# Four layers in one kernel: the second block's attention part in four parts of 256 tokens, its routing in two halves, and the first experts' weights asked for from the counts

## The chip, the core and the metric

The kernel is one program on one core of a Trainium2 chip. A core has five engines with a queue each: TensorE (PE, with its weight loads as PEld) multiplies 128 x 128 blocks into PSUM, VectorE (DVE) and ScalarE (ACT) work elementwise and read PSUM, GpSimd (POOL) works on SBUF and issues the gathers, SyncE (SP) issues most other transfers. Each executes its own queue in order and waits on semaphores for the others. The metric is the device time of one execution in microseconds (us).

## The reference, cut to what matters

x is 16 batches of 64 tokens with 256 features, 1024 tokens in all. Four layers follow one another, each a cross-attention, a second mixing step and a feed-forward step, each added to x:

```python
x = x + _L1_xattn_ref(_layernorm(x), ctx_768, ...)
x = x + _L1_attn_ref(_layernorm(x), ...)
x = x + _L1_ffn_ref(_layernorm(x), ...)
x = x + _L2_xattn_ref(_layernorm(x), ctx_768, ...)
```

The change lies in the second and third of these lines. `_L1_attn_ref`, on its normalized input:

```python
h = _ln(x, ln_conv_g, ln_conv_b)
x = x + conv(h) + conv_b                      # 4 steps back in time, groups of 64 features
h = _ln(x, ln_attn_g, ln_attn_b)
q, k, v = h @ Wq.T + bq, h @ Wk.T + bk, h @ Wv.T + bv
pooled_q = cumsum(q) / (1, 2, ... S)
pooled_k = cumsum(pooled_q * k) / (1, 2, ... S)
x = x + pooled_k * v
h = _ln(x, ln_boom_g, ln_boom_b)
return x + gelu(h @ Wb.T + bb) @ Wu.T + bu
```

`_L1_ffn_ref` sends each token to one of eight experts, the one with the largest softmax probability of `x @ router_W + router_b`: `gate * (relu(x @ W1[e] + b1[e]) @ W2[e] + b2[e])`, with 1024 hidden features. Nothing in either step mixes one batch with another, except that the experts' blocks are filled from all tokens.

## The kernel before

**Layout.** `xs` holds x as eight tiles of 128 tokens x 256 features. TensorE contracts over partitions, so a product needs its input turned to features first: `transposed` (L175) makes two 128 x 128 transposes per tile into PSUM, and another engine evicts them. A float32 product is two instructions in the trace, a transpose is one.

**The stage around the change.** `L1_attn` (L1489) takes each step for all eight tiles before the next step. `norm_x` (L184) normalizes the tiles into `htok` and also evicts their transposes to `hT`, which `L1_attn` does not read. `norm` (L163) does a second normalization into `lnw`, transposes it, and VectorE scales and shifts it into `hp`, which has three columns of zeros ahead of each batch (L1503). The convolution (`ps_conv`, L1514) runs in 512-column products, is turned back and added (`add_by_features`, L1522); another `norm` into `hT` (L1537), q, k, v (`ps_qkv`, L1566), the two running means by scans (`running_mean`, L1554), the sum, another `norm`, the two boom matrices (`ps_hid` L1587, `po` L1591). A normalization of a tile is four VectorE instructions, with one GpSimd power between (`norm_tile`, L150).

**Routing and experts.** `L1_ffn` (L1355) normalizes all tiles (`norm_x`), stores the rows to DRAM for the gather (`keep_row`, L1088, in SP's queue), computes logits (L1010), softmax, the chosen expert, each token's place among those of its expert (`route` L1092, `ranks` L1223). `blocks` (L1245) turns the counts into `rows`, which says where the weights of each block of 128 tokens lie, and with the table of tokens into `tokens`, which says which rows a block gathers. Then eight products add the gate-weighted biases `b2` (L1366 to L1373). Each block (L1374) asks GpSimd for its two weight matrices `wa` and `wb` by `rows` (L1345) and for its tokens `hb` by `tokens` (L1325), three gathers in GpSimd's queue, with three buffers each. Fourteen blocks always run, further ones if the counts need them.

**What sets the order.** Inside `manual_schedule` the named engines' instructions stand in the order of the program text; all other orders are made by a planner with a cost for each instruction. `L1_xattn` before this stage orders TensorE by hand; `L1_attn` and `L1_ffn` are planned throughout. Tiles come from pools; a tile that reuses the memory of an earlier one waits for its readers. `psm` is the PSUM pool of `misc` tiles (two here), `lps` the pool for a layer's own shapes. Weights come through `pack` (L104) into two alternating slots of a ring: attention's weights, the boom matrices, the router's weights with b2 (`pack_L1_gate`), then the next layer's; each pack is asked for when the one before it is taken up.

## Time and profile before

| | us |
|---|---|
| median of 3 runs (2992.84 to 3002.1) | 2994.78 |
| the profiled execution, its own time | 2998.29 |
| its span on the core | 2996.5 |
| attention part, from its first transposes to the last sum into `xs` | 998.35 to 1144.8 |
| logits end, first gather of weights, experts' first transposes | 1158.4, 1172.40, 1189.27 |
| experts' fourteen blocks, end about | 1302 |

Over the span PE is busy 2700.2 us (90%), DVE 1482.1 (49%), ACT 1022.7 (34%), POOL 308.7 (10%); the mean granted TensorE clock is 0.948. These shares are averages over stages with different limits, so the stage from 998 to 1189 has to be read by itself. In the stretches of the trace shown below the first pair is start and end in us from the start of the span, then the length, then the busy time and instruction count of PE, PEld, DVE, ACT and POOL, then the granted clock (1.00 is full speed), the share of the DMA engines that is busy, and GB/s. In the groups, the part between the bars is busy time in us and mean ns of one; the last part is the idle time of the engine ahead of them and what ended it.

### The profile page before, as it was taken

The numbers are of one execution on the slowest core, as the hardware profiler recorded it, in microseconds if no ns is written. First come the engines' busy times: TensorE is split into PE (matmuls) and PEld (weight loads), VectorE is DVE, ScalarE is ACT, GpSimd is POOL, SyncE is SP. The second block draws the span as 40 slices with busy tenths as digits, with TensorE's granted clock in tenths as the row PEclk, the third lists the DMA queues.
The fourth block names the chain that finished last, engine by engine and source line by source line (L and its number), as shares of the span: only waits on it lengthen the run. The fifth ranks groups of instructions, "written<-read, shape, count | busy, mean of one in ns | idle before, by whom it ended". The sixth has DMA issues, their size and how long they took to land. (4 is left out here: it accounts for less than half of the span.)

```text
span 2996.5 us, 42608 instructions
## 1 busy us (share of the span) xinstructions
PE 2700.2 (90%) x16840; PEld 1952.8 (65%) x16840; DVE 1482.1 (49%) x3177; ACT 1022.7 (34%) x2290; POOL 308.7 (10%) x428
## 2 busy tenths in 40 slices
PE   7888997999999788989999998898998898897899
PEld 3566784666666345867777776795776666665668
DVE  3654114666666653234444444314445747658581
ACT  2331122555555211222333322122334455445330
POOL 1112223000000111310101001101001000000000
PEclk9987997999999897989999999899999999998999
DMA  9503771101101003831121112551112222121210
GB/s 241 177 27 144 263 239 50 40 26 32 30 26 33 29 8 135 294 76 46 45 66 45 43 58 70 199 212 63 52 51 88 64 62 73 57 68 53 57 36 7
DMA packets 79220, 253.55 MB, mean 85 GB/s; under 512 B 15151, under 2 KB 26954, under 8 KB 69290
## 3 DMA queue, kind: packets, MB, share of 16 engines
q1 hardware_dynamic: 59562, 165.01, 17.7%
q0 software_dynamic: 13312, 80.28, 7.9%
q10 hardware_dynamic: 6144, 5.51, 0.5%
q8 instruction: 134, 2.20, 0.3%
q14 instruction: 68, 0.56, 0.1%
HBM read 233.80 MB, written 14.82 MB: 83 GB/s over the span
## 5 line engine op out<-in xcount | busy, mean ns | idle before, releaser
L223 DVE TENSOR_REDUCE nmx<-sc 128x1 f32<-128x1024 f32 x264 | 311.8, 1219 | 219.6 <-PE sc L507 134.6
L225 ACT ACTIVATE p<-sc,nmx 128x1024 f32<-128x1024 f32 x264 | 294.6, 1116 | 316.9 <-DVE nmx L223 316.2
L507 PE MATMUL sc<-ctxT,qp 128*128 128x512 f32 (+1 forms) x1024 | 356.0, 602 | 0.0
L507 PEld LDWEIGHTS sc<-ctxT,qp 128*128 128x128 f32 (+1 forms) x1024 | 139.0, 190 | 154.0 <-issue 153.4
L69 PE MATMUL halves<-ctx,pT 128*128 128x192 f32 x1024 | 191.6, 344 | 9.4 <-DVE xs L89 4.0
L69 PEld LDWEIGHTS halves<-ctx,pT 128*128 128x128 f32 x1024 | 179.1, 203 | 12.3 <-DVE xs L89 4.5
L160 POOL TENSOR_TENSOR ln_rs<-ln_ve,nhalf 128x1 f32<-128x1 f32 x120 | 66.9, 562 | 1134.1 <-DVE ln_ve L158 1025.5
L69 PE MATMUL misc<-ctx,pT 128*128 128x192 f32 x1024 | 177.6, 327 | 0.5 <-DVE qT L472 0.5
L235 PE MATMUL ps_t<-ident,p 128*128 128x128 f32 x1088 | 147.8, 278 | 25.3 <-ACT p L225 17.7
L69 PEld LDWEIGHTS misc<-ctx,pT 128*128 128x128 f32 x1024 | 166.3, 191 | 2.1 <-DVE qT L472 1.0
L1938 ACT ACTIVATE da<-rep,al 128x252 f32<-128x252 f32 x256 | 114.7, 498 | 114.8 <-DVE x L1948 98.4
L235 PEld LDWEIGHTS ps_t<-ident,p 128*128 128x128 f32 x1088 | 127.7, 143 | 39.2 <-ACT p L225 22.5
L1948 DVE TENSOR_TENSOR_SCAN x<-da,x 128x512 f32<-128x512 f32 x128 | 152.1, 1213 | 1.9 <-ACT da L1938 1.4
L235 PE MATMUL misc<-ident,p 128*128 128x128 f32 x1024 | 139.8, 283 | 14.2 <-ACT p L225 6.7
L237 ACT COPY pT<-ps_t 128x512 f32<-128x512 f32 x182 | 104.3, 585 | 140.5 <-PE ps_t L235 138.5
L235 PEld LDWEIGHTS misc<-ident,p 128*128 128x128 f32 x1024 | 112.2, 143 | 40.3 <-ACT p L225 13.3
L69 PE MATMUL ps_h<-r,w 128*128 128x256 f32 x512 | 115.3, 385 | 0.0
L237 ACT COPY pT<-misc 128x512 f32<-128x512 f32 x128 | 75.0, 586 | 114.9 <-PE misc L235 114.6
L69 PEld LDWEIGHTS ps_h<-r,w 128*128 128x128 f32 x512 | 97.8, 192 | 16.6 <-issue 2.9
L69 PE MATMUL gu<-dT,wa 128*128 128x128 f32 (+1 forms) x864 | 104.8, 280 | 3.7 <-ACT dT L64 2.4
L239 DVE COPY pT<-misc 128x512 f32<-128x512 f32 x128 | 88.2, 689 | 39.4 <-PE misc L235 28.9
L69 PE MATMUL po<-wb,hid 128*128 128x256 f32 (+1 forms) x440 | 105.6, 387 | 0.0
(472 smaller groups left out, 4437.7 us busy)
## 6 DMA issues: line engine op xcount, KB each, us to landing
ctx<-in_ctx SPq DMA_DIRECT2D x48, 768.0 KB, 4.4
ctxT<-in_ctxT SPq DMA_DIRECT2D x48, 512.0 KB, 4.0
w<-in_L2f_W SPq DMA_DIRECT2D x24, 1024.0 KB, 8.5
rep<-dus SPq DMA_DIRECT2D x256, 64.0 KB, 1.9
ctxT<-in_ctxT SPq DMA_DIRECT2D x16, 768.0 KB, 12.9
ctxT<-in_ctxT SPq DMA_DIRECT2D x96, 128.0 KB, 3.5
ys<-yb ACTq DMA_DIRECT2D x40, 128.0 KB, 4.4
bc_rep<-bcs SPq DMA_DIRECT2D x32, 128.0 KB, 3.0
```

Source lines behind the costliest of these rows:

```text
L69: self.nc.tensor.matmul(out, lhsT, rhs, start=n == 0, stop=n == len(pairs) - 1)
L160: nc.gpsimd.tensor_tensor(rs, ve, self.nhalf, ALU.pow)
L223: self.nc.vector.tensor_reduce(nmx, sc, AX.X, ALU.max, negate=True)
L225: self.nc.scalar.activation(p, sc, AF.Exp, bias=nmx, accum_out=sums)
L235: self.nc.tensor.transpose(ps[:, u, :], p[:, at : at + 128], self.ident)
L237: self.nc.scalar.copy(pT[:, 4 * g : 4 * g + 4, :], ps)
L239: self.nc.vector.tensor_copy(pT[:, 0:4, :], ps)
L507: nc.tensor.matmul(sc[u][:, bass.ts(kh, 512)], qp[n][par][rows, h : h + 2, :].rearrange("p h q -> p (h q)"), ctx[0][rows, at], start=n == ...
L1938: nc.scalar.activation(da[:, g, :, 1:], now[j][:, 0, :].rearrange("p (b s) -> p b s", s=S)[:, :, 1:], AF.Exp, scale=al[:, col : col + 1],)
L1948: nc.vector.tensor_tensor_scan(flat, da.rearrange("p g b s -> p (g b s)"), flat, 0.0, ALU.mult, ALU.add)
```

## The change

`L1_attn` now works on four parts of 256 tokens. Each part is a generator of fifteen steps (`part`), each half of the routing one of five (`routing`), and the string `turns` says whose step comes next: digits 0, 1, 3 and 4 are the four parts, 2 and 5 the routing of the first and the second 512 tokens. TensorE's order is this order (manual). Products have 256 columns. The scale and shift after a normalization, and the biases of k and v, are done by ScalarE during the eviction; a normalization handles two tiles with one GpSimd power. The unread `hT` of the first `norm_x` is gone. `lps` is closed and `misc` has eight PSUM tiles.

Routing, `keep_row` and the bias products move from `L1_ffn` into this layer. `blocks` becomes `block_experts` in two pieces: the first needs only the counts and makes `rows`; it is called after the second half's places have been started and before they are completed. The second makes `tokens`. The first block's weights are gathered by the first `rows`; those of all later blocks by a second tile made from the first and `at`, the lookup's operand. The router's weights load with the boom matrices, and the next layer's weights are asked for at the end of `L1_attn`. Tiles that must outlive the layer move to the `routes` pool. `self.rows` becomes a list with an entry per block. `head` in `pair_masks` shares the memory of `sel`. `gate_bufs`, 4 during `L1_attn`, is the buffer count of the small routing tiles.

```diff
-        head = pool.tile([8, 2, 128], F32, name="head")
-        nc.vector.tensor_copy(head, of)
         mine = pool.tile([8, 2], F32, name="mine")
         sel = pool.tile([8, 2, 2, 128], F32, name="sel")
+        head = sel[:, 1]
+        nc.vector.tensor_copy(head, of)
         for h in range(2):
             nc.vector.tensor_scalar(mine[:, h : h + 1], self.lane[:8], 2.0, float(h), ALU.mult, ALU.add)
             nc.vector.tensor_scalar(sel[:, h], head, mine[:, h : h + 1], None, ALU.is_equal)
...
-    def keep_row(self, i):
-        self.nc.sync.dma_start(self.hs[1 + i * 128 : 1 + (i + 1) * 128], self.htok[:, i, :])
+    def keep_row(self, i, x=None):
+        self.nc.sync.dma_start(self.hs[1 + i * 128 : 1 + (i + 1) * 128], self.htok[:, i, :] if x is None else x)
...
         w2 = self.lp.tile([128, 6 * D], F32, tag="wb" + own, bufs=1 if own else 3, name="wb")
-        self.gather_rows(w2, self.a["L0f_w2r"], self.rows[:, j : j + 1])
+        self.gather_rows(w2, self.a["L0f_w2r"], self.rows[j][:, j : j + 1])
...
@@ -1244,6 +1244,12 @@
     def blocks(self, r, n_blocks):
+        rest = self.block_experts(r, n_blocks)
+        next(rest)
+        next(rest, None)
+    def block_experts(self, r, n_blocks, later=False):
...
-        rows = self.lp.tile([128, n_blocks], I32, name="rows")
+        rows = self.routes.tile([128, n_blocks], I32, tag="rows", name="rows")
         nc.vector.tensor_scalar(rows, of, self.lane, None, ALU.add)
+        self.rows = [rows] * n_blocks
+        yield
         nc.vector.tensor_tensor(past, past, end.unsqueeze(1).to_broadcast(shape), ALU.mult)
         at = self.lp.tile([128, n_blocks], F32, name="at_block")
@@ -1279,18 +1287,25 @@
         nc.vector.tensor_scalar(at, at, self.lane, None, ALU.is_equal)
         ps = self.misc([128, n_blocks])
         self.mm(ps, [(r.table, at[: E * T // 128])])
-        tokens = self.lp.tile([128, n_blocks], I32, name="tokens")
+        tokens = self.routes.tile([128, n_blocks], I32, tag="tokens", name="tokens")
         nc.vector.tensor_copy(tokens, ps)
         first = self.lp.tile([128, E], F32, name="first")
         nc.vector.tensor_tensor(first, end, nb, ALU.subtract)
         nc.vector.tensor_scalar(first, first, 128.0, 1.0, ALU.mult, ALU.subtract)
+        self.tokens = tokens
+        if later:
+            rows = self.routes.tile([128, n_blocks], I32, name="rows_later")
+            behind = self.lp.tile([128, n_blocks], F32, name="behind")
+            nc.vector.scalar_tensor_tensor(behind, at, 0.0, of, ALU.mult, ALU.add)
+            nc.vector.tensor_scalar(rows, behind, self.lane, None, ALU.add)
+            self.rows[1:] = [rows] * (n_blocks - 1)
...
-        return rows, tokens
...
@@ -1335,18 +1350,11 @@
-    def pack_L1_gate(self):
-        self.slot()
-        w, row = self.load("L1f_rW"), self.load_row("L1f_rb")
-        b2 = self.carve(E, D)
-        self.nc.sync.dma_start(b2, self.a["L1f_b2"])
-        return w, row, b2
...
@@ -1354,23 +1362,6 @@
     def L1_ffn(self):
         nc = self.nc
-        rw, rb, b2 = self.pack()
-        self.norm_x()
-        self.routed = r = self.route_setup(1)
-        for i in range(NT):
-            self.keep_row(i)
-        gates = self.gate("gates")
-        for _ in self.route(r, self.gate_logits(rw, rb), 0, gates):
-            pass
-        self.rows, self.tokens = self.blocks(r, L1_BLOCKS)
-        for i in range(NT):
-            pg = self.misc([E, 128])
-            nc.tensor.transpose(pg, gates[:, i, :], self.ident)
-            gT = self.lp.tile([E, 128], F32, tag="gT", bufs=2, name="gT")
-            self.evict(gT, pg)
-            po = self.misc([128, D])
-            self.mm(po, [(gT, b2)])
-            self.add_to_x(i, po)
         def block(j, own=""):
...
@@ -1484,115 +1475,196 @@
     def pack_L1_boom(self):
         self.slot()
-        return self.load("L1a_WbT"), self.load("L1a_WuT"), self.load_row("L1a_bu")
+        boom = self.load("L1a_WbT"), self.load("L1a_WuT"), self.load_row("L1a_bu")
+        gate = self.load("L1f_rW"), self.load_row("L1f_rb")
+        b2 = self.carve(E, D)
+        self.nc.sync.dma_start(b2, self.a["L1f_b2"])
+        return boom, gate, b2
     def L1_attn(self):
         nc = self.nc
-        cv, wq, wk, wv = self.pack()
...
+        (cv, *qkv), ((wb, wu, bu), (rw, rb), b2) = self.pack(), self.pack(ahead=False)
+        self.lps_close()
+        routed, self.gate_bufs = self.route_setup(1), 4
+        later = self.later_steps()
+        def tokens(p, name):
+            return self.lp.tile([128, 2, D], F32, name=f"{name}{p}")
+        def features(p, name):
+            return self.lp.tile([128, 2, CHUNK], F32, name=f"{name}{p}")
+        def normalized(x, out):
+            mv = self.small.tile([128, 2, 2], F32, name="ln_mv2")
+            for t in range(2):
+                st = self.small.tile([128, 6], F32, name="ln_st")
+                nc.vector.bn_stats(st, x[:, t, :])
+                nc.vector.bn_aggr(mv[:, t, :], st)
+            rs = self.small.tile([128, 2], F32, name="ln_rs2")
+            nc.vector.tensor_scalar(rs, mv[:, :, 1], 1e-5, None, ALU.add)
+            nc.gpsimd.tensor_tensor(rs, rs, self.nhalf.to_broadcast([128, 2]), ALU.pow)
+            for t in range(2):
+                nc.vector.tensor_scalar(
+                    out[:, t, :], x[:, t, :], mv[:, t, 0:1], rs[:, t : t + 1], ALU.subtract, ALU.mult
+                )
+        def transposed(x):
+            ps = self.misc([128, 2, CHUNK])
+            for t in range(2):
+                for c in range(2):
+                    nc.tensor.transpose(ps[:, c, bass.ts(t, 128)], x[:, t, c * 128 : (c + 1) * 128], self.ident)
+            return ps
+        def affine(x, to, g, b):
+            ps = transposed(x)
             for c in range(2):
+                src = ps[:, c, :]
+                if len(to.shape) == 4:
+                    src = src.rearrange("p (b s) -> p b s", s=S)
+                nc.scalar.activation(
+                    to[:, c], src, AF.Identity, bias=self.col(b, c), scale=self.col(g, c)
                 )
+        def added(x, to):
+            ps = self.misc([128, 2, D])
+            for t in range(2):
+                for c in range(2):
+                    nc.tensor.transpose(ps[:, t, bass.ts(c, 128)], x[:, c, t * 128 : (t + 1) * 128], self.ident)
+            nc.vector.tensor_tensor(to, to, ps, ALU.add)
+        by_features = [None] * NC
+        def part(p):
+            x = self.xs[:, 2 * p : 2 * p + 2, :]
+            hp = self.lp.tile([128, 2, 4, S + 3], F32, name=f"hp{p}")
+            nc.gpsimd.memset(hp[:, :, :, 0:3], 0.0)
+            x1, w = tokens(p, "x1"), tokens(p, "lnw")
+            normalized(x, x1)
+            normalized(x1, w)
+            yield
+            affine(w, hp[:, :, :, 3:], "L1a_lcg", "L1a_lcb")
+            yield
+            ps = self.misc([128, 2, CHUNK])
+            conv = features(p, "hTs")
             for c in range(2):
                 self.mm(
+                    ps[:, c, :].rearrange("p (b s) -> p b s", s=S),
+                    [(cv[:, c, k, :], hp[:, c, :, k : k + S]) for k in range(4)],
                 )
+            for c in range(2):
+                nc.scalar.activation(conv[:, c, :], ps[:, c, :], AF.Identity, bias=self.col("L1a_conv_b", c))
+            yield
+            added(conv, x1)
+            w = tokens(p, "lnw")
+            normalized(x1, w)
+            yield
+            hT = features(p, "hTs")
+            affine(w, hT, "L1a_lag", "L1a_lab")
+            yield
+            got = []
+            for m, name in zip(qkv, "qkv"):
+                ps = self.misc([128, 2, CHUNK])
+                got.append(features(p, name))
+                for o in range(2):
+                    self.mm(ps[:, o, :], [(m[:, c, o * 128 : (o + 1) * 128], hT[:, c, :]) for c in range(2)])
+                for o in range(2):
+                    nc.scalar.activation(
+                        got[-1][:, o, :], ps[:, o, :], AF.Identity, bias=self.col(f"L1a_b{name}", o)
                     )
+                if name == "q":
+                    yield
+            q, k, v = got
+            inv = self.inv_s.unsqueeze(1).to_broadcast([128, 8, S])
+            for y in (k, v):
+                flat = q.rearrange("p c t -> p (c t)")
+                nc.vector.tensor_tensor_scan(flat, later, flat, 0.0, ALU.mult, ALU.add)
+                steps = q.rearrange("p c (b s) -> p (c b) s", s=S)
+                nc.vector.tensor_tensor(steps, steps, inv, ALU.mult)
+                nc.vector.tensor_tensor(q, q, y, ALU.mult)
+            yield
+            added(q, x1)
+            w = tokens(p, "lnw")
+            normalized(x1, w)
+            nc.gpsimd.tensor_tensor(x, x, x1, ALU.add)
+            yield
+            hT = features(p, "hTs")
+            affine(w, hT, "L1a_lbg", "L1a_lbb")
+            yield
+            if p < 2:
+                g = self.act.tile([128, 8, CHUNK], F32, tag=("htok", "hT")[p], name="hid")
+            else:
+                g = self.lp.tile([128, 8, CHUNK], F32, name=f"hid{p}")
+            for m2 in range(4):
+                ps = self.misc([128, 2, CHUNK])
+                for u in range(2):
+                    m = 2 * m2 + u
+                    self.mm(ps[:, u, :], [(wb[:, c, m * 128 : (m + 1) * 128], hT[:, c, :]) for c in range(2)])
+                for u in range(2):
+                    m = 2 * m2 + u
+                    nc.scalar.activation(g[:, m, :], ps[:, u, :], AF.Gelu, bias=self.col("L1a_bb", m))
+                if m2 % 2:
+                    yield
+            for t in range(2):
                 po = self.misc([128, D])
                 self.mm(
                     po,
                     [(g[:, m, t * 128 : (t + 1) * 128], wu[:, m, :]) for m in range(8)] + [(self.ones[:1, :], bu)],
                 )
+                self.add_to_x(2 * p + t, po)
+                yield
+            o = tokens(p, "x1")
+            normalized(x, o)
+            for t in range(2):
+                self.keep_row(2 * p + t, o[:, t, :])
+            yield
+            by_features[p] = features(p, "hTs")
+            nc.scalar.copy(by_features[p], transposed(o))
+            yield
+        def routing(first):
+            ps = self.misc([128, 4, E])
+            for t in range(4):
+                hT = by_features[(first + t) // 2]
+                self.mm(
+                    ps[:, t, :],
+                    [(hT[:, c, bass.ts(t % 2, 128)], rw[:, c, :]) for c in range(2)] + [(self.ones[:1, :], rb)],
+                )
+            gates = self.gate(f"gates{first}", 4)
+            for piece, _ in enumerate(self.route(routed, ps, first, gates)):
+                if first and not piece:
+                    experts = self.block_experts(routed, L1_BLOCKS, True)
+                    next(experts)
+                yield
+            if first:
+                next(experts, None)
+            yield
+            gTs = []
+            for t in range(4):
+                pg = self.misc([E, 128])
+                nc.tensor.transpose(pg, gates[:, t, :], self.ident)
+                gTs.append(self.lp.tile([E, 128], F32, tag="gT", bufs=4, name="gT"))
+                self.evict(gTs[t], pg)
+            yield
+            for t in range(4):
+                po = self.misc([128, D])
+                self.mm(po, [(gTs[t], b2)])
+                self.add_to_x(first + t, po)
+            yield
+        turns = "0010130134013004314101340301301403101341041134031434234323424242455555"
+        with self.tc.manual_schedule(engines={mybir.EngineType.PE}):
+            parts = [part(0), part(1), routing(0), part(2), part(3), routing(4)]
+            for p in turns:
+                next(parts[int(p)])
+        self.start_pack(self.at)
+        self.routed, self.gate_bufs = routed, 1
...
             "L1_attn": (self.L1_attn, [self.pack_L1_attn, self.pack_L1_boom]),
-            "L1_ffn": (self.L1_ffn, [self.pack_L1_gate]),
+            "L1_ffn": (self.L1_ffn, []),
             "L2_xattn_attn": (self.L2_xattn_attn, [lambda: self.pack_heads64("L2"), self.pack_L2_attn]),
...
                 tc.tile_pool(
-                    name=f"psm_{name}", bufs=3 if name == "L1_xattn" else 2, space=PSUM, reuse_waits="tile"
+                    name=f"psm_{name}", bufs={"L1_xattn": 3, "L1_attn": 8}.get(name, 2), space=PSUM, reuse_waits="tile"
                 ) as self.ps_misc,
```

## The prediction

> **What bounds the kernel now.** I first cut the stage that the diff rewrites into stretches (busy time per engine; the last three numbers are TensorE's granted clock, the DMA share and GB/s). The stage is the second block's attention part and the routing, from 998.3 us to the experts' first instruction at 1189.3.
>
> ```profile
> 998.30:1009.90 11.60, 5.43 (x24) 2.69 (x24) 9.85 (x39) 1.49 (x4) 3.30 (x6) 0.77 0.47 182
> 1009.90:1031.00 21.10, 19.89 (x56) 9.44 (x56) 7.90 (x30) 2.75 (x4) 1.74 (x4) 0.88 0.00 1
> 1031.00:1046.00 15.00, 9.45 (x27) 4.29 (x26) 12.45 (x45) 0.69 (x1) 4.24 (x8) 0.77 0.00 0
> 1046.00:1070.00 24.00, 19.78 (x55) 8.55 (x54) 22.92 (x35) 3.34 (x4) 2.70 (x4) 0.99 0.01 1
> 1070.00:1081.00 11.00, 3.55 (x12) 1.81 (x13) 8.07 (x29) 0.00 (x0) 5.53 (x10) 0.50 0.00 0
> 1081.00:1127.20 46.20, 46.20 (x144) 26.14 (x143) 11.71 (x40) 10.31 (x15) 3.81 (x7) 0.98 0.04 12
> 1144.40:1158.50 14.10, 12.46 (x64) 11.10 (x64) 3.07 (x9) 2.77 (x5) 0.55 (x1) 0.74 0.46 160
> 1158.50:1172.40 13.90, 5.87 (x23) 4.70 (x23) 10.93 (x60) 0.26 (x1) 0.00 (x1) 0.50 0.00 1
> 1172.40:1189.30 16.90, 12.74 (x27) 5.16 (x27) 4.87 (x20) 1.02 (x4) 8.53 (x9) 0.50 0.89 329
> ```
>
> PE (first) and DVE (third) take turns: whenever DVE is near full (1031, 1070, 1158), PE is under two thirds busy and its clock falls to half; while PE is full (1081 to 1127), DVE does a quarter. All 1024 tokens go through each step together, so nothing else can fill a normalization. Next, the groups of instructions, for what PE waits on (last column) and the price of pooling:
>
> ```profile
> L179 PE MATMUL misc<-ident,lnw 128*128 128x128 f32 x48 | 12.8, 372 | 17.9 <-DVE lnw L170 10.7 <-DVE ln_mv L156 3.7 <-DVE ln_ve L158 3.5
> L1556 DVE TENSOR_TENSOR_SCAN pk<-later,pq 128x512 f32<-128x512 f32 x4 | 4.9, 1224 | 0.1
> L1557 DVE TENSOR_TENSOR pk<-pk,inv_s 128x512 f32<-128x512 f32 x4 | 2.8, 692 | 0.1
> ```
>
> Last, the order in time around the experts' start:
>
> ```profile
> 1172.40 1.00 POOL L1312 DMA_INDIRECT wa<-in_L1f_W1b,rows  x1 [25.68 <-DVE first L1286]
> 1175.00 0.95 POOL L1312 DMA_INDIRECT hb<-hs,tokens  x1 [0.36 <-ACT gT L64]
> 1188.12 1.22 PE L69 MATMUL misc<-w,gT 8*128 8x256 f32 x2 [0.40 <-DVE gT L62]
> 1189.27 0.69 PE L179 MATMUL misc<-ident,hb 128*128 128x128 f32 x2
> ```
>
> Weights and tokens are asked for at 1172 to 1175, but the experts start only when PE has finished the eight bias products (`gT`), one every 1.9 us at half clock. Afterwards (1189 to 1302) PE is full; I leave that stage as it is.
>
> **TensorE's work after the change.** Durations are spacings in the trace at full clock: a 512-column pass 0.43 us, a 256-column pass 0.214 (15 weight loads in 3.21 us), a transpose 0.13 (four in about 0.5). Half as many columns per pass costs nothing, since 0.19 us of weight load still fits under 0.214. Each product is two passes.
> - Convolution 64 x 0.214 = 13.7; q, k, v 96 x 0.214 = 20.5; first boom matrix 128 x 0.214 = 27.4; second, eight tiles at 4.27 (1131.43 to 1135.70) = 34.2; transposes 96 x 0.13 = 12.5 (16 fewer: the unused `hT` of L188 goes). Together 108.3, or 27 per part.
> - Routing of the first half: logits four tiles x 0.85 = 3.4, ranks 0.9, table 8 x 0.22 = 1.8, gate transposes 0.4, bias products 2.0: 8.5, between turns of the parts.
> - Logits of the second half, 3.4.
>
> That is 120.2 us up to the end of the last logits, if PE never waited; the stretches above spend 160.1 on it (998.3 to 1158.4).
>
> **Waits that stay.** A two-tile normalization from its input to its output is 3.0 us (one tile: 1131.99 to 1133.96 is 2.0; the second adds 0.6 of statistics and 0.41 of scaling). VectorE's part of it is 2.15.
> - Start: two normalizations in a row for part 0 lie between 998 and its first transpose. They cost 0 if done during the attention before, 6 if not. No tile of this pool was written before 993.62 (`hp`'s memset) or 998.35 (`later`), so I take 5.
> - The next turns of part 0 wait for ScalarE (two 0.37 to 0.4 us evictions and the signals, 1.2 a time), with little of other parts yet: 3.
> - Middle: I counted, in the turns, the PE work between each turn and the one it feeds. After pooling it is 6.6, 6.6, 8.7 and 7.7 us against 5.2 of VectorE (2 x (1.22 + 0.69 + 0.69)) plus about 1; after the additions that follow, 4.4 at the least against 0.7 + 3.0 + 0.6. It fits only if VectorE takes each up at once. Its load from 998 to the last logits is 20 normalizations x 2.15 = 43, pooling 4 x 5.2 = 21, sums 9, routing 9: 82 of some 140. A wait in its queue is not shown by the trace of before; nearest is the row above, 17.9 us over 24 tiles, 0.75 each. For 16 chains I take 0.5 each, 8 us; the bounds are 0 and 16 x 2.6 = 42 (half a pooling ahead of each).
> - End: part 3's last normalization and transposed copy have only 2.4 us of PE work for cover: 2.6; ranks and table of the first half, 2.
> - Half clock at the start and in the last logits: 3.
>
> Sum 23.6: the last logits end at 998.35 + 120.2 + 23.6 = 1142.2 instead of 1158.4.
>
> **From there to the experts.** Before: 30.9 us (to 1189.27). After: softmax and largest 3.2, running counts of four tiles instead of eight 1.0, the product with ones 0.9, nine small operations to `rows` 2.2: `rows` at +7.3 instead of +13.7. POOL then asks for `wa` and `wb` at +7.6 and +8.9, landed at about +15.5 (2.1 MB at the 400 GB/s of 1172 to 1189). Behind them in POOL's queue stands `hb`, and behind it every later block's gathers: they wait for the tokens. Ranks, 16 column operations (3.6), table at half clock and `tokens` end at +14.4, `hb` is asked for at +15.3, landed at +18.8. PE has four gate transposes and four bias products after +14: 4 x 0.4 + 4 x 1.2 and 0.5 put the experts' first transpose at **+21**. So PE sets this end and the early weights are hidden: asked for 4 us later they would still be in time. Of the 9.9 us won here, 7.7 are the four bias products already done.
> Experts' start: 1142.2 + 21 = 1163.2, that is 26.1 earlier.
>
> **Edits costed at nothing.** `head` shares `sel`'s room: once per set-up, the same operations, in place. The affine evictions (L1503 and L1537, 48 x 0.40 = 19 us) and the biases of k and v go from VectorE to ScalarE, where they lie beside other parts' work. Moved tiles and added buffers issue nothing; the two extra operations for later rows are 0.4 us in the shadow of the table product. SP: gate weights (16 KB) ride with the boom load at 998, hidden until turn 26; eight `keep_row` stores (128 KB, 1.7 us to land) are spread out, the last well ahead of +15. The next stage's 2.4 MB gets its slot when part 3's k and v are done, so lands before the gathers; if it collided it would take 5 to 6 us of their time, which is all the 5.5 us that `wa` has to spare. POOL: 20 powers for 40, four two-tile sums.
> Table loads: the row of L1036 and of L1588 is 1.28 us each. The first half's Exp falls among part 3's Gelus, two switches more: 2.6. The Trainium skill (ScalarE: Activation LUTs, What ACT_TABLE_LOAD costs) puts a switch at 2.66 us with its drain, and would have all work of one set done together: 5.3 against this change. ScalarE has some 38 us of work in 140 (22 in the stretches before, and 40 more evictions at 0.4) and neither lies right ahead of a PE turn, so both sums are nothing; uncovered, 2.6 to 5.3.
> The clock: the rows give 0.50 where PE had short work among gaps (1070, 1158) and 0.98 to 1.00 where dense. The skill (TensorE: Matmul & The Clock Gate, HAM oscillation) asks for no PE gap above some 3.4 us; the turns leave none in the middle. By the row for the first block's hand-ordered stage (60 to 200 us: mostly 1.00, dips to 0.66 and 0.83) I could lose 8% of 108, 9 us; by the rule nothing. I take the rule, and keep the 9 us for the range.
>
> **Sum.** 2998.29 (the profiled execution, 1.8 around its span of 2996.5) - 26.1 = 2972.2. The median of the runs is 3.5 below that execution: **2968.7**, its own range 2958 to 2980.
>
> **Rivals.**
> - *Denser*, 0.22: first normalizations done ahead and hardly any queueing, 8.6 us of waits for 23.6: 2954. For it: VectorE is only 60% busy in the attention's tail. Against: the late memsets.
> - *The early request is held*, 0.12: `wa` lies over memory that L1_attn reads until its last bias product. POOL then stands still to about +20, weights land at +28, the start is at +30: 2978. Against: the pool's first tiles are those of early steps.
> - *Order without overlap*, 0.10: VectorE's planned order puts chains in series so that PE gains a few us only: 2985 to 2992.
> - *Slower*, 0.11: a wait on VectorE replaces the old ones. PE's order is fixed, so one late normalization stops all four parts. It decides at 26.1/16 = 1.6 us per chain above my 0.5; with a pooling's second half and part of another normalization ahead of each (3.6) it is 16 x 3.1 = 50 us: 3018. For it: the lack of slack counted above. Against: VectorE has 60 us free.
> - The rest, 0.45, is the forecast.
>
> From no change a measurement tells about 0.3%, 9 us. Faster: 0.45 + 0.22 + 0.12 and half of the fourth = 0.84; same 0.05; slower 0.11. The range 2950 to 2989 leaves out the slower case, half of the fourth and some 4 in 100 below.
>
> **What would show it.** Last logits near 1142 and the experts' first transpose about 21 us later; clock near 1.0 from 1010 to 1130; `wa` asked for some 7 us ahead of `hb`; PE waiting for `lnw` by under 10 us in all. Wrong would be: PE idle before `misc` for VectorE over 30 us, `wa` waiting on a bias product, or another stage moving by over 5.

## The result, and the profile after

The changed kernel takes **2959.9 us** (median of 4 runs, 2952.71 to 2962.49) where the kernel before, on the same chip, takes 2996.03 (2992.84 to 3002.1): a ratio of 0.987, 95% interval 0.984 to 0.989. (The 2994.78 of the table ahead is the median of the first three of its runs.) The forecast was 2968.7, with a range of 2950 to 2989. The sign was right and the time lies in the range; the gain is 36 us where 26 were forecast.

All of it lies in the stage that was rewritten. The last product of the cross-attention ends at 997.8 us before and at 998.1 now; the experts' first transposes stand at 1153.0 instead of 1189.3, 36.3 us earlier, and the span is 36.0 shorter. The experts' blocks after that take 112.5 us instead of some 112.7.

The stretches of the changed kernel, with the columns of those shown before:

```profile
997.80:1012.00 14.20, 8.92 (x29) 6.38 (x29) 9.52 (x41) 2.45 (x6) 3.48 (x5) 0.59 0.42 150
1012.00:1035.00 23.00, 22.83 (x118) 19.71 (x118) 17.26 (x47) 9.85 (x23) 4.27 (x6) 1.00 0.00 1
1035.00:1040.00 5.00, 2.72 (x17) 2.25 (x16) 4.46 (x11) 2.59 (x6) 2.84 (x2) 1.00 0.00 0
1040.00:1128.60 88.60, 87.61 (x412) 72.52 (x412) 40.18 (x122) 29.36 (x63) 9.39 (x11) 0.96 0.10 33
1128.60:1135.30 6.70, 6.61 (x28) 6.22 (x28) 0.65 (x3) 1.87 (x2) 0.00 (x0) 0.52 0.11 39
1135.30:1153.00 17.70, 8.88 (x28) 5.94 (x28) 10.95 (x64) 0.74 (x3) 6.30 (x8) 0.50 0.44 156
1153.00:1265.50 112.50, 107.94 (x706) 98.60 (x708) 22.60 (x63) 27.82 (x77) 33.72 (x36) 0.97 0.82 277
```

PE and DVE no longer take turns. From 1012 to 1035 both are busy at once, and from 1040 to 1128.6 PE has 87.6 us of work in 88.6. What stays are a start of 14 us, a hole before 1040, and the two rows at half clock: the second half's logits (1128.6 to 1135.3) and the chain from there to the experts.

The groups that answer to those shown before, over the same stage:

```profile
L1519 PE MATMUL misc<-ident,lnw 128*128 128x128 f32 x48 | 7.8, 297 | 6.7 <-DVE lnw L1510 6.7
L1585 DVE TENSOR_TENSOR_SCAN q<-later,q 128x512 f32<-128x512 f32 x8 | 9.8, 1223 | 6.2 <-ACT q L1576 6.1
L1587 DVE TENSOR_TENSOR q<-q,inv_s 128x512 f32<-128x512 f32 x8 | 5.8, 724 | 0.2
```

The 48 transposes of normalized tiles waited 17.9 us; now they wait 6.7, in two places. A scan of the pooling costs what it did, 1.22 us. All that PE waits for between the attention's end and the last logits (total, times, longest):

```profile
PE misc L1519 <- DVE lnw L1510: 6.7, 2, 4.4
PE misc L1519 <- DVE x L1510: 1.0, 1, 1.0
PE misc L69 <- ACT hp L1528: 0.9, 2, 0.7
```

That is 8.6 us: 4.4 at the start and 0.9 for the first `hp`, 2.3 before 1040, 1.0 ahead of the last part's final transposes. Last, the order in time around the experts' start (start, duration, what it waited for):

```profile
1143.16 1.07 POOL L1327 DMA_INDIRECT wa<-in_L1f_W1b,rows  x1 [2.05 <-DVE s_row L1118]
1147.81 0.95 POOL L1327 DMA_INDIRECT hb<-hs,tokens  x1 [2.33 <-DVE tokens L1291]
1148.20 3.78 PE L69 MATMUL misc<-w,gT 8*128 8x256 f32 x8
1153.01 0.69 PE L179 MATMUL misc<-ident,hb 128*128 128x128 f32 x2 [1.04 <-DMA hb<-hs,tokens]
```

PE is done with the bias products (`gT`) at 1151.98 and then waits 1.04 us for the tokens to land. From issue to landing the first block's weights took (last number, us):

```profile
wa<-in_L1f_W1b,rows POOLq DMA_INDIRECT x1, 5.6
wb<-in_L1f_W2r,rows POOLq DMA_INDIRECT x1, 8.1
```

`wb` was asked for at 1144.53, so it landed at about 1152.6, just ahead of the tokens. In the kernel before, PE did not wait for the tokens: there the bias products ended last.

### The profile page after: what moved, and what is told of

It reads as the page before. It is cut to its first block, busy times and chain, and to the rows that moved or that the text cites. A ratio compares the mean times of both kernels' runs of the same rounds, so it can differ in the third digit from the quotient of the medians.

```text
span 2960.5 us, 42845 instructions
## 1 busy us (share of the span) xinstructions
PE 2687.8 (91%) x16972; PEld 1979.6 (67%) x16972; DVE 1462.2 (49%) x3117; ACT 1045.9 (35%) x2353; POOL 302.6 (10%) x407
## 5 line engine op out<-in xcount | busy, mean ns | idle before, releaser
L235 PE MATMUL ps_t<-ident,p 128*128 128x128 f32 x1088 | 146.8, 277 | 25.3 <-ACT p L225 17.6
L237 ACT COPY pT<-ps_t 128x512 f32<-128x512 f32 x182 | 104.3, 585 | 139.3 <-PE ps_t L235 137.2
L160 POOL TENSOR_TENSOR ln_rs<-ln_ve,nhalf 128x1 f32<-128x1 f32 x80 | 45.1, 569 | 725.8 <-DVE ln_ve L158 676.0
L69 PEld LDWEIGHTS ps_h<-r,w 128*128 128x128 f32 x512 | 97.8, 192 | 16.6 <-issue 2.9
L69 PEld LDWEIGHTS gu<-dT,wa 128*128 128x128 f32 (+1 forms) x864 | 98.4, 185 | 10.9 <-ACT dT L64 4.8
## 6 DMA issues: line engine op xcount, KB each, us to landing
ctxT<-in_ctxT SPq DMA_DIRECT2D x16, 768.0 KB, 14.1
```

The source lines that it names most:

```text
L69: self.nc.tensor.matmul(out, lhsT, rhs, start=n == 0, stop=n == len(pairs) - 1)
L160: nc.gpsimd.tensor_tensor(rs, ve, self.nhalf, ALU.pow)
L235: self.nc.tensor.transpose(ps[:, u, :], p[:, at : at + 128], self.ident)
L237: self.nc.scalar.copy(pT[:, 4 * g : 4 * g + 4, :], ps)
```

## Experiments

Executions already differ before this stage begins (in these profiles the attention's last product ends between 994.7 and 1005.9 us, and at 1010.1 with the first norms ahead), so the kernels are compared by three marks of their own profile: the end of the attention's last product, VectorE's first reading of the second half's logits (in the kernel before, of all logits), and the experts' first transposes of `hb`.

| kernel | attention's end to logits | logits to experts | both | time, median us |
|---|---|---|---|---|
| before | 160.9 | 30.6 | 191.4 | 2996.0 |
| changed | 137.2 | 17.7 | 154.9 | 2959.9 |
| steps together | 168.1 | 18.0 | 186.1 | 2992.2 |
| routing at the end | 148.0 | 18.6 | 166.6 | 2971.7 |
| weights behind the lookup | 137.2 | 21.8 | 158.9 | 2970.3 (one run) |
| scale and shift on VectorE | 142.2 | 18.6 | 160.8 | 2967.1 (one run) |
| pooling doubled | 145.3 | 18.0 | 163.3 | 2970.2 (one run) |
| first norms ahead | 128.7 | 17.6 | 146.3 | 2963.9 |
| second weights last | 137.2 | 16.6 | 153.8 | 2969.7 (one run) |
| three PSUM tiles | 137.8 | 18.2 | 156.1 | 2959.1 (one run) |
| logits between turns | 136.7 | 18.4 | 155.1 | 2970.0 (one run) |
| three together | 128.1 | 17.2 | 145.3 | 2957.1 |

The times of one run carry the scatter of the earlier stages; the marks are what to read there. The part from the logits to the experts takes 17.6 to 18.6 us in the eight kernels that leave it alone. In each of them PE ends it waiting for the tokens, which come 5.1 to 6.1 us after they are asked for; differences of up to 1 us there are scatter. The kernel before took 3001.7 us in the runs beside the first four of these, 2998.4 beside the next four and 2996.3 beside the last two, so the ratios below, not the times, compare the sets.

### The same parts, not set apart in time

The products stay in parts of 256 tokens, but the four parts take each step one after another.

```diff
-        turns = "0010130134013004314101340301301403101341041134031434234323424242455555"
+        turns = "0134013401340134013401340134013401340134013400110130123324242342455555"
```

> The changed kernel with only its order string altered: all four parts take each of the first eleven steps (up to the second half of the first boom matrix) before the next step, as the kernel before did; the end of the string is kept in its form. Theory A (the gain in the attention part is VectorE's chains lying beside other parts' products): between an addition and the next normalized transposes only 4 us of transposes cover 4 x 2.85 us of VectorE, twice, the first normalizations lie bare and the poolings end late: TensorE idles 30 to 45 us before the last logits instead of 8.6, these end 20 to 40 us later than 1135, the time is 2980 to 3000. Rival B (the gain came from the smaller edits: evictions on ScalarE, one power for two tiles, the unread transposes dropped, routing in halves): last logits within 8 us of 1135 and a time under 2968.

The experts come 31.2 us later than in the changed kernel, and the ratio to the kernel before is 0.9975 (0.9965 to 0.9985). PE's waits from the attention's end to the logits:

```profile
PE misc L1519 <- DVE lnw L1510: 30.2, 12, 4.4
PE misc L1537 <- DVE q L1588: 2.1, 1, 2.1
```

All twelve transposes of `lnw`, three for each part, now wait for their normalization. Of the 30.9 us up to the logits, 24.6 are waits (33.2 against 8.6). The remaining 6.3 lie in TensorE's work itself, which is the same products: it runs at a lower clock where the waits are (two stretches, columns as above):

```profile
1025.00:1045.00 20.00, 13.52 (x64) 11.03 (x63) 9.04 (x32) 6.46 (x14) 2.76 (x4) 0.74 0.00 0
1065.00:1085.00 20.00, 9.53 (x33) 7.32 (x34) 10.63 (x34) 6.20 (x11) 8.10 (x8) 0.57 0.26 98
```

Dividing into parts, together with the smaller edits, wins nothing by itself here: up to the logits this kernel is 7.2 us slower than the one before. The offset in time is what the attention part's gain lives on. The shorter way from logits to experts (18.0 for 30.6) is all that this version has over the kernel before.

### The first half's routing at the end

```diff
-        turns = "0010130134013004314101340301301403101341041134031434234323424242455555"
+        turns = "0010130134013004314101340301301403101341041134031434343344442222255555"
```

> The changed kernel with the first half's five routing turns taken out of the parts and put between the last turn of part 3 and the second half's routing. Theory A (routing in halves beside the parts is worth its whole chain): the last logits of the second half come some 12 to 18 us later than 1135 and the experts' first transposes as much later than 1153; time 2972 to 2978. Rival B (only the 8.5 us of TensorE work move and the chain is covered anyway): experts' start within 4 us, time 2960 to 2964.

11.7 us later at the experts, just under the 12 to 18 of theory A, and 10.9 of it before the last logits; ratio 0.991 (0.989 to 0.992). The routing's own chain now stops PE, at the ranks and at the table:

```profile
PE misc L69 <- DVE route L1051: 2.5, 1, 2.5
PE misc L69 <- DVE s_col L1126: 2.2, 1, 2.2
```

From 1120.5 to 1145.4, where these products lie, the granted clock is 0.52. Doing the first half's routing among the parts is worth about a third of the gain.

### The first block's weights behind the lookup

```diff
-            self.rows[1:] = [rows] * (n_blocks - 1)
+            self.rows = [rows] * n_blocks
```

> The changed kernel with the first block's weights, too, gathered by the later rows, which are made behind the lookup's operand. The prediction's view (TensorE's bias products set the experts' start and the early weights are hidden): first transposes within 1 us of 1153. Rival (the tokens stand behind the weights' 2.1 MB in the transfers and that landing sets the start): weights asked for about 3 us later and the first transposes 3 us later, 1156.

The gathers around the start in this kernel:

```profile
1151.53 1.02 POOL L1327 DMA_INDIRECT wa<-in_L1f_W1b,rows_later  x1 [5.68 <-DVE route_table L1136]
1154.11 0.95 POOL L1327 DMA_INDIRECT hb<-hs,tokens  x1 [0.30 <-issue]
...
1161.79 0.69 PE L179 MATMUL misc<-ident,hb 128*128 128x128 f32 x2 [5.09 <-DMA hb<-hs,tokens]
```

The weights are asked for 11.5 us after the logits' mark instead of 7.9, the tokens behind them at 14.1 instead of 12.5, and PE waits 5.1 us for the tokens instead of 1.0. The experts start 4.0 us later, where the rival had said 3. The forecast had said that the early request is hidden and that 4 us later would still be in time. That is wrong.

### The scale and shift back on VectorE

```diff
-                nc.scalar.activation(
-                    to[:, c], src, AF.Identity, bias=self.col(b, c), scale=self.col(g, c)
+                nc.vector.tensor_scalar(
+                    to[:, c], src, self.col(g, c), self.col(b, c), ALU.mult, ALU.add
```

> The changed kernel with the scale and shift after a normalization done by VectorE, as before the change, instead of ScalarE: 24 instructions of some 0.42 us, 10 us more for VectorE. Theory A (VectorE has room to spare and TensorE sets the pace): last logits no more than 3 us later than 1135. Rival (the move to ScalarE is what makes the interleaving fit): 8 us or more later.

Logits 5.0 us later, experts 5.9: between what the two theories said. The new waits are nearly all in the first 35 us:

```profile
PE misc L69 <- DVE hp L1528: 5.5, 4, 1.7
PE misc L69 <- DVE hTs L1528: 1.0, 2, 0.6
```

`hp` is the convolution's input; each of the four parts waits for its own once, between 1006 and 1033. While the parts have their first normalizations behind one another, PE waits for VectorE; after 1048 it waits for no scaling.

### Twice the pooling on VectorE

Two more scans per `q*y` that leave the values as they are, some 20 us of VectorE in all.

```diff
+        nil = self.lp.tile([128, 512], F32, name="nil")
+        nc.vector.memset(nil, 0.0)
...
+                for _ in range(2):
+                    nc.vector.tensor_tensor_scan(flat, nil, flat, 0.0, ALU.mult, ALU.add)
```

> The changed kernel with four more scans per part that leave the values as they are, in VectorE's chain of the pooling: 4 x 1.22 = 4.9 us more for each part, 20 us in all. Theory A (the order string covers each pooling just about, as counted: 6.6 to 8.7 us of products against 5.2 and a start of 1): TensorE waits 2 to 5 us more in each part, the stretch from the attention's last product to the last logits grows from 137.2 us by 10 to 18. Rival B (there is much slack, and the forecast's 8 us of queueing were missing because VectorE could be late without harm): it grows by less than 4.

Experts 8.4 us later, logits 8.1: between the two theories (10 to 18, and under 4). PE's waits up to the logits are 15.1 us for 8.6, the larger ones:

```profile
PE misc L1521 <- DVE lnw L1512: 7.1, 3, 5.1
PE misc L1539 <- DVE q L1592: 6.1, 3, 3.2
```

Of some 5 us more in each of four poolings, PE sees 2.0, 3.2 and 0.8 in three of them and nothing in one. The order by hand therefore leaves about 2 to 5 us of slack at each pooling, taken one after another (a wait at one moves PE back and eases the next). The forecast's own count leaves 0.4 to 2.5 there (6.6 to 8.7 us of products against 6.2).

### The first normalizations ahead

Parts 0 and 1 put their normalized tiles into memory of the block's own pool that is free during the attention, so they need not wait for the layer's pool.

```diff
-            x1, w = tokens(p, "x1"), tokens(p, "lnw")
+            if p < 2:
+                room = self.act.tile([128, NT, D], F32, tag=("htok", "hT")[p], ...)
+                x1, w = room[:, 0:2, :], room[:, 2:4, :]
+            else:
+                x1, w = tokens(p, "x1"), tokens(p, "lnw")
```

> The changed kernel with the first two normalized tiles of parts 0 and 1 in the rooms of htok and hT, which are free during the attention before, instead of the layer's own pool, whose first writes come after that attention's last product. Theory A (memory freed late is what holds part 0's first normalization): TensorE's first wait of 4.4 us falls under 1, last logits 132 to 134 us after the attention's last product instead of 137.2, time 4 us less. Rival B (VectorE's planned order holds it, or its work moved forward slows the attention by as much): 136 or more.

The wait at the start falls from 4.4 to 0.5 us and the way to the logits is 8.5 shorter, so the memory that came free late was its cause. Of the 8.5, 3.9 are this wait, 2.5 the first convolution, now at full clock (3.7 for 6.2 us), 1.3 the 24 passes that stand at 1040 in the changed kernel, at full clock here too, and 0.8 the transposes just ahead of these two. The time, though, is 0.988 (0.986 to 0.991) of the kernel before, like that of the changed kernel. Where the rest went is seen in the attention ahead. Its 64 last projections, one line for the changed kernel (range of durations, first start to last start):

```profile
L69 PE MATMUL misc<-w,ym x64: 379/379/631, 595.4 to 997.5; 128*128 128x256 f32 x64
```

and the same line for this one:

```profile
L69 PE MATMUL misc<-w,ym x64: 379/379/483, 602.6 to 1009.7; 128*128 128x256 f32 x64
```

From the first to the last of these the attention takes 407.1 us for 402.1; in the other profiles of this study it takes 401.9 to 403.5, the last kernel below apart. The gain at the start was paid for ahead of it, by 5 us: from the first of these projections to the experts' first transposes it is 553.8 us for 557.6, so 3.8 us are left, too little for the time to tell. That VectorE's and ScalarE's extra work there is what delays it was not tried by itself.

### The first block's second weight matrix last

The first block's tokens are gathered between its two weight matrices; `wb` takes rows that depend on the lookup.

```diff
-        self.gather_rows(w2, self.a["L1f_W2r"], self.rows[j][:, j : j + 1])
+        if not j:
+            hb = self.block_rows(j, own)
...
+        self.gather_rows(w2, self.a["L1f_W2r"], self.rows_w2[j][:, j : j + 1])
```

> The changed kernel with the first block's second weights (wb) asked for behind its tokens, by rows made from the looked-up tokens; the first weights stay early. If the tokens wait for the weights' transfer ahead of them, they now stand behind one matrix of 1.05 MB: they land before the bias products end, and the experts' first transposes come 16.7 us after the last logits instead of 17.7, with no wait on the tokens' landing. If a gather simply takes that long, 17.5 or more.

```profile
1150.65 1.07 POOL L1330 DMA_INDIRECT wa<-in_L1f_W1b,rows  x1 [2.04 <-DVE s_row L1118]
1155.76 0.95 POOL L1330 DMA_INDIRECT hb<-hs,tokens  x1 [4.05 <-DVE rows_later L1304]
1157.02 0.94 POOL L1330 DMA_INDIRECT wb<-in_L1f_W2r,rows_later  x1 [0.30 <-PE misc L69]
...
1159.39 0.69 PE L179 MATMUL misc<-ident,hb 128*128 128x128 f32 x2
```

The tokens are asked for 0.5 us later after the logits than in the changed kernel (13.0 for 12.5), yet PE no longer waits for them: it takes them up 3.6 us after the request, where in the changed kernel they took 5.2. So in the changed kernel the tokens did stand behind the 2.1 MB of weights. 1.1 us are won, as theory forecast, and that is 1.0 below the shortest of the kernels that leave this part alone; it is too little for the time to tell.

### Three PSUM tiles instead of eight

```diff
-                    name=f"psm_{name}", bufs={"L1_xattn": 3, "L1_attn": 8}.get(name, 2), space=PSUM, ...
+                    name=f"psm_{name}", bufs={"L1_xattn": 3, "L1_attn": 3}.get(name, 2), space=PSUM, ...
```

> The changed kernel with three PSUM tiles instead of eight for the layer's shared shape. Theory A (depth in PSUM is needed for the interleaving, as two or three parts have results waiting for ScalarE or VectorE): the stretch to the last logits grows from 137.2 us by 5 to 15. Rival B (evictions are prompt and eight are more than it needs): by 1 at most.

0.7 us more to the logits, 1.2 to the experts, of which 0.5 lie in the part that scatters by 1: rival B. Five of the eight tiles could be given away.

### The first half's logits between other turns

```diff
-        turns = "0010130134013004314101340301301403101341041134031434234323424242455555"
+        turns = "0010130134013004314101340301301403101341041134031423242324323424242455555"
...
+                if not first and t < 3:
+                    yield
```

> The first half's logits (8 columns per product) are taken one tile at a time between other parts' turns, in place of four tiles in a row; nothing else moves and nothing is left out. Theory: some 3 us of such short products on end are what lowered the clock at 1105 in the changed kernel, so with 0.9 us at a time the granted clock stays at 1.00 from 1045 to the last transposes, the 16-pass product that took 5.1 us takes 3.6, and the last logits come 1.5 us sooner after the attention's end (135.7 for 137.2). The dip at the start, the one after the 2.3 us wait near 1040 and the one in the last logits stay. Rival (the clock falls there for another reason, such as a window of its own or what ran in the microseconds before): one product near 1105 to 1115 still takes about 5 us, and the last logits stay at 137 +- 0.5.

In the changed kernel the clock falls during these products although PE has no gap (PE from 1101.7 on, first the logits, then the boom product behind them; columns as above):

```profile
1045.00:1101.70 56.70, 56.70 (x273) 47.58 (x272) 25.47 (x59) 21.05 (x47) 7.31 (x8) 1.00 0.13 47
1101.70:1105.50 3.80, 3.80 (x27) 3.58 (x26) 0.00 (x0) 2.12 (x3) 0.00 (x0) 0.93 0.00 0
1105.50:1110.60 5.10, 5.10 (x18) 4.02 (x17) 2.45 (x15) 1.51 (x2) 0.00 (x0) 0.72 0.00 0
```

With 0.8 us of them at a time it does not fall (the stretch that holds all four tiles):

```profile
1053.00:1121.00 68.00, 68.00 (x331) 56.96 (x329) 28.19 (x72) 25.33 (x54) 7.99 (x9) 1.00 0.12 41
```

The 16-pass product that took 5.13 us takes 3.7. The dip was there, after 2.5 to 3.3 us of short products on end, in all seven kernels that have them in that place, and is gone where they stand elsewhere or apart (with the routing at the end, the clock is 1.00 from 1045 to 1115). The logits came 0.5 us sooner, not 1.5: the softmax now has one turn less of cover, and PE waits 0.7 us for it. The experts came no sooner at all (155.1 for 154.9), since PE then waited 1.75 us for the tokens instead of 1.04.

### Three of these together

First norms ahead, second weights last and logits between turns in one kernel.

> Three edits together: parts 0 and 1 have their first normalizations in memory that is free during the attention (as in the run with the first norms ahead), the first block's tokens are gathered ahead of its second weight matrix, and the first half's logits stand between other turns. Theory: each keeps its own price, so from the attention's end to the experts' first transposes 154.9 becomes about 154.9 - 8.5 - 1.1 - 1.5 = 143.8; the attention is again some 5 us longer, so 6 us are left of it: ratio 0.985 beside 0.987 for the changed kernel, less than the intervals tell apart. Rival (the parts share one cover, so the gains do not add): 147 or more to the experts, ratio 0.987 to 0.988.

145.3 us to the experts, between the forecast sum (143.8) and the rival's 147. That sum took the 1.5 us that the logits between turns had been expected to win. With what each edit won by itself up to the experts, 8.6, 1.1 and -0.2, it is 145.4: the prices do add. The attention takes 407.1 us again, as in the run with the first norms ahead. The median is 2957.1 (2952.9 to 2963.7), 0.987 (0.985 to 0.989) of the kernel before: not to be told from the changed kernel.

## Why the prediction was right, and where not

**Work and waits up to the logits: forecast 143.8, measured 137.2.** PE waits 8.6 us. Half clock costs some 9.0: four products over their length at full clock (the first convolution 6.2 for 3.7 us, the 24 passes after 1040 6.7 for 5.3, the 16 at 1105 5.1 for 3.6, the second half's logits 6.0 for 3.4), 8.0 together, and 1.0 in the transposes just ahead of three of them. That leaves 119.6 for TensorE's work, so the forecast's 120.2 stands. The waits and the clock, term by term:

- Start, 5 + 3: measured 4.4 + 0.9. The choice of a late start, read off the late memsets, was right; with room elsewhere the 4.4 falls to 0.5.
- Middle, 16 chains x 0.5 = 8: measured one wait of 2.3. **This is the term that was mis-sized most.** The row it was taken from, 0.75 us a tile, came from a stage in which nothing else stood behind a normalization. In the new order a late VectorE result first eats slack, about 2 to 5 us at a pooling as the doubled pooling showed. The working had counted 0.4 to 2.5 there and next to none behind the additions (4.4 against 4.3).
- End, 2.6 + 2: measured 1.0. The ranks and the table of the first half cost PE nothing.
- Half clock, 3: measured 9.0, wrong the other way.

So the mechanism was right (set the steps apart, and PE fills), and the run with the steps together shows it: 24.6 us of waits come back. Two readings behind it were too strong. VectorE and TensorE did not take turns in every row: from 1046 to 1070 VectorE is 95% busy, TensorE 82%, at a clock of 0.99, and from 1031 to 1046 the clock is 0.77, not half. And the nearness of the time is in part luck: the half clock gave back 6.0 of the 12.0 us by which the waits were overestimated.

The rival *denser*, 2954, is nearer to the measured 2959.9 than the forecast is. Its hardly any queueing came true; its first normalizations ahead did not. Its 8.6 us held half clock too, so what answers to it is 17.6; that PE's waits alone are also 8.6 is chance. *Slower* fell: VectorE's 20 us of extra work cost 8, far from 50. *Order without overlap* did not come; its time, 2985 to 2992, is what the kernel with the steps together takes, there by TensorE's order and not by VectorE's. *Early request held* fell: `wa` was asked for 0.9 us after `rows` was written. The trace names a later instruction of the routing (`s_row`) as its releaser, so 0.9 is the most that it was held.

**The clock.** The Trainium skill (TensorE: Matmul & The Clock Gate, HAM oscillation) was taken at its word, that no PE gap below some 3.4 us costs the clock. Neither dip in the middle has such a gap, and the measurement decides. One dip follows a wait of 2.3 us. Eight kernels have this same wait with the same 24 passes behind it: in five these run at half clock, in three at full speed. The changed kernel, then the one with three PSUM tiles:

```profile
1040.00 1.00 PE L1519 MATMUL misc<-ident,lnw 128*128 128x128 f32 x4 [2.28 <-DVE lnw L1510]
1040.80 6.69 PE L69 MATMUL misc<-hTs,w 128*128 128x256 f32 x24
...
1041.06 0.67 PE L1519 MATMUL misc<-ident,lnw 128*128 128x128 f32 x4 [2.29 <-DVE lnw L1510]
1041.56 5.34 PE L69 MATMUL misc<-hTs,w 128*128 128x256 f32 x24
```

The other dip has no gap at all, only 8-column products on end. Together they cost some 3 of the 9 us that the first block's row would have allowed; the rest of the 9.0 is at the two ends, where PE had waited or has only short work.

**From the logits to the experts: forecast 21, measured 17.7.** `rows` was written at +6.8 to +7.0 (forecast 7.3) and `wa` was asked for at +7.9 (7.6). The column operations, table and lookup took less than forecast, so that `hb` was asked for at +12.5 (15.3), and the bias products took 0.94 us each (1.2), ending at +16.7. The step that failed is "PE sets this end and the early weights are hidden". The weights landed at about +17.3, not +15.5 (the working took 400 GB/s from a row that prints 329). `hb`, which stands behind them, needed 5.2 us to land, not 3.5, and its landing set the start at +17.7. Requested later, the weights delay the tokens by 4 us. The working had seen this queue and, with a longer PE chain, left it off the path. Of the 12.9 us won in this part, the early request is shown to be worth 4.0; that the rest is the first half's ranks and bias products done earlier is read from the trace and was not tried by itself.

**Costed at nothing.** ScalarE's scalings (beyond the 0.9 us counted at the start), the table loads (four of 1.28 us lie in the stage, at 1045, 1103, 1106 and 1130, two more than before, and PE waits behind none of them) and the loads on SyncE's queue cost nothing that can be seen; the next layer's weights moved between 1082 and 1091, ahead of the gathers, as reckoned. Moving the scalings off VectorE, costed as hidden, is worth 6 us, and without it the cover is missing in the first 35 us.

Against the forecast the waits are 12.0 us shorter, the half clock 6.0 longer, TensorE's work 0.6 shorter and the last part 3.3 shorter: about 10 us together, which is what the gain was larger by. Of the signs that it named, PE's wait for `lnw` (6.7 us, under 10) held; `wa` stood 4.7 us ahead of `hb` and not 7.

## What to carry to other kernels

When steps that feed one another are cut into parts, try what the cut earns without an offset in time: here it earned nothing until the parts were set apart. Count what slack the order leaves, because a queue's delay is paid only beyond it. A request moved forward is worth reading together with what stands behind it in its own queue: here the early weights paid off through the tokens queued after them. Undoing parts of the change singly (31, 12, 4 and 6 us here) added up to 53 us, more than the 36 that the change won, so such prices overlap; three further edits at different waits did add (145.4 us by the sum, 145.3 measured). A wait taken away at one end may be paid for in the stage that took the work over.

## What the runs showed of the hardware that was not expected

- Products of 8 columns back to back lower the granted clock after 2.5 to 3.3 us although the profile shows no gap on PE (0.72 from 1105.5 to 1110.6); at 0.8 us at a time they do not (1.00).
- One and the same wait of 2.3 us is followed by half clock in five kernels (24 passes in 6.7 us) and by full clock in three (5.3 us). The runs do not show what decides it.
- A gather of one block's tokens took 5.1 to 6.1 us to land behind two weight matrices asked for shortly ahead of it in its queue, and at most 3.6 behind one that had been asked for 5 us earlier.
